# Attention with masked tokens: context of one slot block in four as three float16 products, row additions moved to GpSimd, leaner buffers

## The chip, the cores and the metric

The kernel runs on one core of a Trainium2 chip. TensorE (PE in the profile; its weight loads are PEld) multiplies matrices from SBUF into PSUM. VectorE (DVE), ScalarE (ACT) and GpSimd (POOL) work on tiles of 128 partitions, and SyncE (SP) issues transfers. Every engine takes its own instructions in order and waits for the others by semaphores. The metric is the device time of one execution in microseconds. Three timed runs of the kernel before took 1044.49, 1047.27 and 1048.94 us, a median of 1047.27 us.

## The reference

There are 16 batches of 512 features by 1024 tokens, with a mask of zeros and ones for each batch, 8 heads of 64, and queries that serve as keys and values too.

```python
xt = jnp.transpose(x, (0, 2, 1))
q = xt @ Wq.T
qh = q.reshape(B, T, NH, dk).transpose(0, 2, 1, 3)
scores = scale * jnp.einsum('bhqd,bhkd->bhqk', qh, qh)
logits = (scores * cmask + (1.0 - cmask) * NEG) * rmask
attn = jax.nn.softmax(logits, axis=-1)
ctx = jnp.einsum('bhqk,bhkd->bhqd', attn, qh)
out = ctx.transpose(0, 2, 1, 3).reshape(B, T, D) @ Wo.T
return x + transpose(out)
```

A masked key gets no weight. A masked query has logits of zero throughout, so that its context is the mean of all values, one row for the whole batch.

## The kernel before

**Work is kept to the active tokens.** About half of a batch's 1024 tokens are active (502 to 539). The kernel sorts them on the chip into slots: `slots` and `index` make for each batch a list of rows, and GpSimd gathers rows of x by an indirect transfer (`rows`, L395). A batch has four slot blocks of 128 and a tail of up to 32 slots; the width A of a batch is 544 (batches 0 to 4), 528 (5 to 13) or 512 (14 and 15). The masked rows get only the mean's row added: they are gathered (`late`), the row `ub` is added (`rest`, L888, on VectorE), and they are scattered to the output (`scatter_now`, L901).

**Stages of a batch.** `xt` transposes the gathered rows on TensorE and splits them into a high and a low float16 part (L444, L445). `query` multiplies with the split weights in three float16 products (L513). `qsplit` splits the queries in the same way into `hl` (L529, L530), copies the high part behind the low one (L531), and four SP transfers (`spread`) bring high and low over each other into `xx`, so that one score needs two products. `value` transposes the queries into `v`, four blocks of 128 slots by 128 (two heads), and takes their squares for the softmax shift; `bottom` turns the largest square into `nm`, the negative shift of each head. `scores` makes one block (128 slots by A) of one head in two PSUM buffers (L701), and ScalarE takes the exponential into a float32 tile `p` and sums it (L705). The symmetry of scores makes this block its own transpose, so it can be used as it is.

**Context.** `attend` multiplies the values of a block with the exponentials of that block and accumulates over the blocks into `pav` (L726): for each half g of the columns (A/2 each) and each head k of a pair, a float32 product of 128 rows, 64 columns of weights and A/2 moving columns. The two heads go to the two halves of the array's columns. The tail's part comes last (L730). Then ScalarE copies `pav` out (L734), `norm` scales and splits it (L799 to L807), `project` multiplies with the output weights (L817), `plus` adds the result to the gathered rows (L822), and GpSimd scatters them.

**Order.** The loop in `run` goes over the batches; within one over 16 pairs (p, i) of a pair of heads p and a block i, with two more places for the tails. At each place the scores of head 2p and of head 2p+1 are made, and `fill` puts units of other stages between them, from a list with costs: projection of the batch before, queries of the batch after, and so on. The context of the four blocks of a pair is made in one group, at the place i = 1 of the next pair, in the order of blocks 3, 2, 1, 0. One transfer of GpSimd is issued at each place (`issue`); it, and the additions of L888, wait for the most recent product of TensorE at the time of writing (`beat`), which paces them. The framework then orders each engine's instructions by its own estimate; `behind` and `high_priority` are hints to it.

**Buffers** that matter here: two in PSUM for scores (`pss`), two small ones in PSUM (`pm`) that queries, projections, transposes and values share, 12 tiles `p`, 6 tiles `v`, 2 tiles `hl` with three parts.

**A guard.** The shift must lie between MMIN and MMAX, the counts of active tokens between 384 and A, and so on (`ok`); otherwise a general path computes the whole again.

Of the kernel before, what the change touches and what calls it, by code (L numbers as in the profile page):

```python
# [10 lines left out]
F32 = mybir.dt.float32  # L11
# [8 lines left out]
P = 128  # L20
D = 512
# [15 lines left out]
MMAX = 60.0  # L37
# [6 lines left out]
HPO = 300  # L44


class Fast:
# [45 lines left out]
    def setup(self, mask_t):  # L93
# [30 lines left out]
        self.oht = fixed("oht", [P, B, TB, NB], F16)  # L124
# [11 lines left out]
        self.qt = fixed("qt", [P, 2, HG, CT])  # L136
        self.number = iota("number", [P, B - 2], [[1, B - 2]], 2, 0)
# [70 lines left out]
    def permute(self):  # L208

        nc, B = self.nc, self.B - 2  # L210
        at, mh = self.at16, self.later16
        each = self.sb([P, B, TB, B], F16, "ch", 2)
        nc.vector.tensor_tensor(each, at.unsqueeze(2).broadcast_to([P, B, TB, B]),
                                mh.rearrange("p b j -> p j b").unsqueeze(1).broadcast_to([P, B, TB, B]), ALU.mult)
        with nc.allow_low_precision(reason="one of the terms is 0 or 1, the others are 0"):
            nc.vector.tensor_reduce(self.later16, each, AX.X, ALU.add)
# [15 lines left out]
    def slots(self, b0, b1):  # L232
# [13 lines left out]
        for j in range(TB):  # L246
# [22 lines left out]
                                self.ionb.unsqueeze(1).broadcast_to([P, NC, NB]), ALU.is_equal)  # L269
        for b in range(B):  # L270
            nc.vector.tensor_tensor(self.oht[:, b0 + b], oh[:, b * TB:(b + 1) * TB, :],
                                    self.tok.unsqueeze(2).broadcast_to([P, TB, NB]), ALU.mult)
# [46 lines left out]
    def index(self, b):  # L319
        nc = self.nc  # L320
        s = self.st[b]
        ol = s["ol"]
        pi = self.pm([P, NB])
        for j in range(TB):
            self.pe = nc.tensor.matmul(pi, lhsT=ol[:, j, :], rhs=self.oht[:, b, j, :], start=(j == 0), stop=(j == TB - 1)).ins
# [78 lines left out]
    def gather_now(self, b, j):  # L404
        s = self.st[b]
        if j < 4:
            s["xa"].append(self.rows(s["idx"][:, j:j + 1], self.sb([P, D], F32, "xa", 13)))
        else:
            s["xt"] = self.rows(s["idx"][:s["A"] - 512, 4:5], self.sb([P, D], F32, "xt"))
# [64 lines left out]
    def xt(self, b, k):  # L474
# [4 lines left out]
        if n:  # L479
            x = s["xa"][k] if k < 4 else s["xt"]  # L480
            if b == 0:
                pt = self.ps_s.tile([P, 2, D], F32, tag="s", name="pss")[:, 0, :DC * n].rearrange("p (c n) -> p c n", c=DC)
            else:
                pt = self.pm([P, DC, n])
            for c in range(DC):
                self.pe = nc.tensor.transpose(pt[:, c, :], x[:n, c * P:(c + 1) * P], self.ident[:n, :n]).ins
# [34 lines left out]
    def qsplit(self, b, e):  # L521
# [5 lines left out]
        full = self.sb([P, 3, C], F16, "hl", 2)  # L527
# [3 lines left out]
        nc.vector.tensor_copy(hl[:, 2, :], hl[:, 0, :])  # L531
# [6 lines left out]
        def spread():  # L538
            lo, up = slice(0, DK), slice(DK, P)
            nc.sync.dma_start(out=xx[lo, 0:2, :], in_=hl[lo, 0:2, :])  # L540
            nc.sync.dma_start(out=xx[up, 0:2, :], in_=hl[lo, 1:3, :])
            nc.sync.dma_start(out=xx[lo, 2:4, :], in_=hl[up, 0:2, :])
            self.last_xx = nc.sync.dma_start(out=xx[up, 2:4, :], in_=hl[up, 1:3, :]).ins
# [15 lines left out]
    def value(self, b, e):  # L559
# [72 lines left out]
    def bottom(self, b, g):  # L632
# [6 lines left out]
        nc.vector.tensor_scalar(nm[:, :HG], pb, -SCALE, None, ALU.mult)  # L639
# [4 lines left out]
        nc.vector.tensor_scalar(okm, nm[:, :HG], -MMAX, None, ALU.is_ge)  # L644
        nc.vector.scalar_tensor_tensor(okm, nm[:, :HG], -MMIN, okm, ALU.is_le, ALU.mult)
# [15 lines left out]
    def scores(self, b, p, i):  # L661
# [8 lines left out]
        if i is None:  # L670
# [8 lines left out]
            t = self.sb([P, C], F32, "p", 12)[:, :A]  # L679
# [24 lines left out]
        t = self.sb([P, C], F32, "p", 12)[:, :A]  # L704
# [3 lines left out]
        return t  # L708

    def attend(self, b, p, i, ps):  # L710
# [6 lines left out]
        for g in range(2):  # L717
            for k in (1, 0) if i < 4 else range(2 if A == C else 1):
                cols = slice(g * CH, (g + 1) * CH)
                if i < 4:  # L720
                    with ExitStack() as st:
                        if self.group_first:

                            st.enter_context(self.behind(self.group_first))
                            st.enter_context(self.tc.high_priority(offset=HPO))
                        mm = nc.tensor.matmul(s["pav"][k * DK:(k + 1) * DK, g, :CH], lhsT=s["v"][p][:, i, k * DK:(k + 1) * DK],  # L726
                                              rhs=ps[k][:, cols], start=(i == 3), stop=(i == 0 and A == 512))
                    self.group_first = self.group_first or mm.ins
                elif A > 512:
                    nc.tensor.matmul(s["pav"][:, g, :CH], lhsT=s["vt"][p // 2][:, k, p % 2 * 2:p % 2 * 2 + 2, :],  # L730
                                     rhs=s["pt"][:, p % 2, cols], start=False, stop=(k == 1 or A < C))
        if i == 4:
# [44 lines left out]
    def norm(self, b, p):  # L777
# [4 lines left out]
        if p == 0:  # L782

            s["ch"] = self.sb([P, NP, 512], F16, "ch", 2) if b < self.B - 1 else self.xh[:, :, :512]
            s["cl"] = self.sb([P, NP, 512], F16, "cl", 2) if b < self.B - 1 else self.xl[:, :, :512]
# [15 lines left out]
        ch, cl = s["ch"][:, p, :], s["cl"][:, p, :]  # L801
# [7 lines left out]
    def product(self, ch, cl, cols, po=None, es=range(DC)):  # L809
# [5 lines left out]
        for e in es:  # L815
            for k, (a, w) in enumerate(((ch, wh), (ch, wl), (cl, wh))):
                nc.tensor.matmul(po[:cols.stop - cols.start], lhsT=a[:, e, cols], rhs=w[:, e, :],  # L817
# [14 lines left out]
    def late(self, b, j, tag="xi", bufs=8):  # L832

        self.post(lambda: self.late_now(b, j, *(("xg", 1) if j == 4 else (tag, bufs))), urgent=j == 4)

    def late_now(self, b, j, tag, bufs):
        s = self.st[b]
        idx = s["tails"][:len(self.group[b]) * CT] if j == 4 else s["idx"][:P if j < 8 else T - self.kept[b] - 3 * P, j:j + 1]
        s.setdefault("xi", {})[j] = self.rows(idx, self.sb([P, D], F32, tag, bufs)), idx

    def project_tail(self, b, *part):
# [6 lines left out]
        po = self.product(*s["ct"], slice(0, m), *part)  # L848
# [8 lines left out]
    def project_means(self, b):  # L857
# [9 lines left out]
        po = self.product(m[:, 0], m[:, 1], slice(0, n))  # L867
# [14 lines left out]
    def rest(self, b, j):  # L882
        s = self.st[b]

        def add():
            x, idx = s["xi"][j]
            n = idx.shape[0]
            self.once(self.nc.vector.tensor_tensor(x[:n], x[:n], s["ub"][:n], ALU.add), self.beat)  # L888
# [414 lines left out]
```

## Time and profile before

| | |
|---|---|
| median of three timed runs | 1047.27 us (1044.49 to 1048.94) |
| the profiled execution's own time | 1036.56 us |
| its span, first to last instruction | 1034.9 us |
| granted TensorE clock, mean | 0.993 |
| TensorE busy | 989.3 us, 96% |
| VectorE busy | 724.1 us, 70% |
| ScalarE busy | 659.2 us, 64% |
| GpSimd busy | 301.5 us, 29% |

The span is cut into instructions of each engine. A busy TensorE is not the same as a TensorE at its peak, because its products overlap: a product's recorded duration is the time from its start to the arrival of its result, and the distance between the starts of two products is what each really costs. "Idle before" is the time that the engine stood still right before the instructions of a group, and the name behind the arrow is what ended it. A line Lnnn is a line of the kernel's source. In the list of waits the name before the arrow waited for the name behind it; then come us in total, times, and the longest.

### The profile page before, as it was taken

The page shows a single profiled execution, that of the slowest core. Times are in us where ns is not written, and L with a number is a line of the kernel's source. Part 1 is how long each engine was busy: PE and PEld are TensorE (multiplying, and loading weights), DVE is VectorE, ACT ScalarE, POOL GpSimd, SP SyncE. Part 2 cuts the span into 40 slices and gives each one's busy share as a digit, 9 for nine tenths or more (in the row PEclk, how much of TensorE's full clock was granted, in tenths as well). Part 3 has the DMA queues.
Part 4 walks back from the last instruction along what each step waited for, and adds up shares of the span by engine and source line. Part 5 has one row for each costly group of instructions (what it writes and reads, how often), then busy time and mean ns, then how long its engine had stood idle before and what let it go on. Part 6 is the DMA issues. An engine that isn't in the chain of part 4 may idle for free. (4 is left out here: it accounts for less than half of the span.)

```text
span 1034.9 us, 23506 instructions
## 1 busy us (share of the span) xinstructions
PE 989.3 (96%) x8455; PEld 686.2 (66%) x8455; DVE 724.1 (70%) x2410; ACT 659.2 (64%) x1702; POOL 301.5 (29%) x307
## 2 busy tenths in 40 slices
PE   7798999999999999999999999999999999999996
PEld 6576667666676766767666676766767666676563
DVE  6897668676675667876676787767677776666653
ACT  5876667657667665667667567666667666565550
POOL 3101013222311232333232333323233232326562
PEclk9899999999999999999999999999999999999998
DMA  6846556557654485575658665576665657455652
GB/s 206 224 135 184 139 137 162 174 160 205 175 133 131 138 244 167 154 208 142 197 158 217 181 174 170 155 202 187 164 211 147 195 166 193 140 142 186 195 187 85
DMA packets 78795, 177.73 MB, mean 172 GB/s; under 512 B 14688, under 2 KB 20576, under 8 KB 78672
## 3 DMA queue, kind: packets, MB, share of 16 engines
q1 hardware_dynamic: 57584, 108.40, 39.0%
q0 software_dynamic: 21088, 67.75, 20.9%
q8 instruction: 69, 1.13, 0.5%
q14 instruction: 54, 0.44, 0.1%
HBM read 91.49 MB, written 33.91 MB: 121 GB/s over the span
## 5 line engine op out<-in xcount | busy, mean ns | idle before, releaser
L705 ACT ACTIVATE p<-pss,nm 128x528 f32<-128x528 f32 (+2 forms) x512 | 359.3, 706 | 186.5 <-PE pss L701 176.6
L701 PE MATMUL pss<-xx 128*128 128x264 f16 (+2 forms) x2048 | 302.7, 277 | 6.3 <-ACT p L705 5.2
L726 PE MATMUL pav<-p,v 128*64 128x264 f32 (+2 forms) x2048 | 243.3, 390 | 0.0
L701 PEld LDWEIGHTS <-xx 128*128 128x128 f16 x2048 | 194.9, 99 | 64.2 <-issue 26.2
L726 PEld LDWEIGHTS pav<-p,v 128*64 128x64 f32 x2048 | 141.5, 137 | 85.6 <-issue 13.5
L901 POOL DMA_INDIRECT y_out<-xa,idx x68 | 73.5, 1081 | 282.3 <-PE pss L701 100.1
L513 PE MATMUL pm<-xh,wqh 128*128 128x264 f16 (+5 forms) x512 | 142.4, 278 | 3.7 <-DVE xa L822 3.1
L513 PE MATMUL pm<-xh,wql 128*128 128x264 f16 (+5 forms) x512 | 141.9, 277 | 0.0
L513 PE MATMUL pm<-xl,wqh 128*128 128x264 f16 (+5 forms) x512 | 141.8, 277 | 0.0
L395 POOL DMA_INDIRECT xa<-x_in,idx x68 | 67.4, 992 | 208.2 <-PE pss L701 91.8
L513 PEld LDWEIGHTS <-wqh 128*128 128x128 f16 x1024 | 98.3, 99 | 23.7 <-issue 7.1
L705 ACT ACTIVATION_READ_ACCUMULATOR p<-pss,nm 128x1 f32 x512 | 104.1, 203 | 0.0
L901 POOL DMA_INDIRECT y_out<-xi,idx x60 | 73.6, 1226 | 96.7 <-PE pss L701 27.6
L817 PE MATMUL pm<-woh,ch 128*128 128x512 f16 x240 | 91.1, 380 | 0.0
L817 PE MATMUL pm<-wol,ch 128*128 128x512 f16 x240 | 91.0, 379 | 0.0
L817 PE MATMUL pm<-woh,cl 128*128 128x512 f16 x240 | 91.0, 379 | 0.0
L395 POOL DMA_INDIRECT xi<-x_in,idx x60 | 62.5, 1042 | 93.6 <-PE pss L701 31.2
L516 ACT ACTIVATE q<-pm 128x264 f32<-128x264 f32 (+5 forms) x128 | 50.1, 391 | 58.1 <-PE pm L513 57.4
L822 DVE SCALAR_TENSOR_TENSOR xa<-pm,xa 128x512 f32<-128x512 f32 x60 | 41.3, 688 | 54.3 <-PE pm L817 50.6
L817 PEld LDWEIGHTS <-ch 128*128 128x128 f16 x480 | 46.0, 98 | 44.8 <-issue 0.9
L888 DVE TENSOR_TENSOR xi<-xi,ub 128x512 f32<-128x512 f32 (+1 forms) x60 | 40.8, 687 | 42.6 <-PE pss L701 42.3
L799 DVE TENSOR_TENSOR c<-c,rb 128x528 f32<-128x528 f32 (+2 forms) x64 | 45.4, 709 | 30.0 <-PE pm L513 16.3
(223 smaller groups left out, 1506.4 us busy)
## 6 DMA issues: line engine op xcount, KB each, us to landing
xx<-hl SPq DMA_DIRECT2D x224, 136.0 KB
xm<-x_nat_in SPq DMA_DIRECT2D x56, 512.0 KB
rb<-rd SPq DMA_DIRECT2D x72, 132.0 KB
rb<-rd SPq DMA_DIRECT2D x40, 136.0 KB
pt<-c SPq DMA_DIRECT2D x36, 132.0 KB
pt<-p SPq DMA_DIRECT2D x36, 132.0 KB
ub<-ud SPq DMA_DIRECT2D x16, 256.0 KB
xx<-hl SPq DMA_DIRECT2D x32, 128.0 KB
```

What stands on the lines that cost most here:

```text
L395: dma = self.nc.gpsimd.indirect_dma_start(out=tile[:n], out_offset=None, in_=self.x, in_offset=bass.IndirectOffsetOnAxis(ap=idx, axis=0))
L513: self.beat = nc.tensor.matmul(pq, lhsT=w[:, c, e * P:(e + 1) * P], rhs=xx[:, c, cols], start=(k == 0), stop=(k == 3 * DC - 1)).ins
L516: nc.scalar.activation(s["q"][:, e, cols], pq, AF.Copy, scale=1.0 / (SX * SW))
L701: self.beat = nc.tensor.matmul(pt[:, g, :CH], lhsT=xx[:, 2 * k, i * P:(i + 1) * P], rhs=xx[:, 2 * k + a, g * CH:(g + 1) * CH], start=(a == ...
L705: self.exp = [nc.scalar.activation(t.rearrange("p (g c) -> p g c", g=2), pt[:, :, :CH], AF.Exp, bias=s["nm"][p // HG][:, p % HG:p % HG + 1 ...
L726: mm = nc.tensor.matmul(s["pav"][k * DK:(k + 1) * DK, g, :CH], lhsT=s["v"][p][:, i, k * DK:(k + 1) * DK], rhs=ps[k][:, cols], start=(i == ...
L799: self.once(nc.vector.tensor_tensor(c[:, :A], c[:, :A], s["rb"][p], ALU.mult), self.beat if p < 3 else None)
L817: nc.tensor.matmul(po[:cols.stop - cols.start], lhsT=a[:, e, cols], rhs=w[:, e, :], start=(e == 0 and k == 0), stop=(e == DC - 1 and k == 2))
L822: self.nc.vector.scalar_tensor_tensor(x, po, 1.0 / (SX * SW), x, ALU.mult, ALU.add)
L888: self.once(self.nc.vector.tensor_tensor(x[:n], x[:n], s["ub"][:n], ALU.add), self.beat)
L901: dma = self.nc.gpsimd.indirect_dma_start(out=self.out, out_offset=bass.IndirectOffsetOnAxis(ap=idx, axis=0), in_=x, in_offset=None)
```

## The change

*Context of block 0.* The exponent gets a constant of 26 ln 2 added (LIFT), so the exponentials of all blocks are 2^26 times as large; the correction for empty slots and the sums carry the same factor. For block 0 alone (PARTS), the exponential t is split: ph is t/2048 in float16, on VectorE for even heads and on ScalarE for odd ones, and pl is 2048 ph - t in float16, on VectorE. The value's block 0 is split in `parts`: 2048 v in float16 (ScalarE, out of PSUM), the rest of 2048 v (VectorE), and the negative high part over 2048 (GpSimd). The context of block 0 then is three float16 products in place of a float32 one: high value by ph, low value by ph, negative high value by pl. Blocks 1, 2, 3 and the tail stay as they were.

*Row additions.* The addition of the mean's row to the masked rows (`rest`) goes from VectorE to GpSimd, in line with its transfers.

*Buffers.* 10 tiles `p` for 12; `hl` without the copy of the high part, which two of the four spreading transfers replace by reading the two parts in reverse order; the one-hot tables in two buffers of four batches for one of 16; `ch` and `cl` in six tiles of one pair each; one tile `xgt` for the tails' rows of both kinds, in different partitions; the permutation of masks in two halves. New tiles: `ph` and `pl` (4 each) and `vp` (6).

*Guard.* MMAX goes from 60 to 20.

```diff
-MMAX = 60.0
+MMAX = 20.0
+LIFT = 26.0 * math.log(2.0)
+UP = 2048.0
+PARTS = (0,)
...
-        full = self.sb([P, 3, C], F16, "hl", 2)
+        full = self.sb([P, 2, C], F16, "hl", 2)
...
-        nc.vector.tensor_copy(hl[:, 2, :], hl[:, 0, :])
...
-            nc.sync.dma_start(out=xx[lo, 0:2, :], in_=hl[lo, 0:2, :])
-            nc.sync.dma_start(out=xx[up, 0:2, :], in_=hl[lo, 1:3, :])
+            nc.sync.dma_start(out=xx[lo, 0:2, :], in_=hl[lo])
+            nc.sync.dma_start(out=xx[up, 0:2, :], in_=turned(hl[lo]))
...
+        s.setdefault("vp", []).append(self.parts(v, pv))
...
+    def parts(self, v, pv):
+        nc = self.nc
+        n = len(PARTS)
+        t = self.sb([P, 3, n, P], F16, "vp", 6)
+        nc.scalar.activation(t[:, 0], pv[:, :n], AF.Copy, scale=UP)
+        nc.vector.scalar_tensor_tensor(t[:, 1], v[:, :n], UP, t[:, 0], ALU.mult, ALU.subtract)
+        nc.gpsimd.tensor_scalar(t[:, 2], t[:, 0], -1.0 / UP, None, ALU.mult)
+        return t
...
-        nc.vector.tensor_scalar(nm[:, :HG], pb, -SCALE, None, ALU.mult)
+        nc.vector.tensor_scalar(nm[:, :HG], pb, -SCALE, LIFT, ALU.mult, ALU.add)
...
-        t = self.sb([P, C], F32, "p", 12)[:, :A]
+        t = self.sb([P, C], F32, "p", 10)[:, :A]
...
-        return t
+        if i not in PARTS:
+            return t
+        hi, lo = (self.sb([P, C], F16, k, 4)[:, :A] for k in ("ph", "pl"))
+        if p % 2:
+            nc.scalar.activation(hi, t, AF.Copy, scale=1.0 / UP)
+        else:
+            nc.vector.tensor_scalar(hi, t, 1.0 / UP, None, ALU.mult)
+        nc.vector.scalar_tensor_tensor(lo, hi, UP, t, ALU.mult, ALU.subtract)
+        return hi, lo
...
+            terms = [(v[:, i], ps)]
+            if i in PARTS:
+                terms = [(vp[:, j, i], [h[j // 2] for h in ps]) for j in range(3)]
+            for g in range(2):
+                for j, (w, r) in enumerate(terms):
+                    for k in (1, 0):
...
+                            mm = nc.tensor.matmul(s["pav"][k * DK:(k + 1) * DK, g, :CH], lhsT=w[:, k * DK:(k + 1) * DK],
+                                                  rhs=r[k][:, cols], start=(i == 3),
+                                                  stop=(i == 0 and A == 512 and j == len(terms) - 1))
...
-            self.once(self.nc.vector.tensor_tensor(x[:n], x[:n], s["ub"][:n], ALU.add), self.beat)
+            with self.behind(*(() if self.pool and self.pool[0] in self.scatters else self.pool)):
+                i = self.nc.gpsimd.tensor_tensor(x[:n], x[:n], s["ub"][:n], ALU.add)
+            self.once(i, self.beat)
```

More of the change, by code (lines that the diff above doesn't have):

```diff
@@ L211, in permute @@
         at, mh = self.at16, self.later16
[L212 to L216, printed above, removed]
+        parts = []
+        for k in range(2):
+            n = B // 2
+            each = self.sb([P, n, TB, B], F16, "tmp", 2)
+            nc.vector.tensor_tensor(each, at[:, k * n:(k + 1) * n].unsqueeze(2).broadcast_to([P, n, TB, B]),
+                                    mh.rearrange("p b j -> p j b").unsqueeze(1).broadcast_to([P, n, TB, B]), ALU.mult)
+            parts.append(each)
+        for k, each in enumerate(parts):
+            with nc.allow_low_precision(reason="one of the terms is 0 or 1, the others are 0"):
+                nc.vector.tensor_reduce(mh[:, k * n:(k + 1) * n], each, AX.X, ALU.add)
     def active(self, b0, b1):
@@ L324, in index @@
         for j in range(TB):
-            self.pe = nc.tensor.matmul(pi, lhsT=ol[:, j, :], rhs=self.oht[:, b, j, :], start=(j == 0), stop=(j == TB - 1)).ins
+            self.pe = nc.tensor.matmul(pi, lhsT=ol[:, j, :], rhs=self.oht[b][:, j, :], start=(j == 0), stop=(j == TB - 1)).ins
         s["idx"] = self.sb([P, NB], I32, "idx", 7)
@@ L408, in gather_now @@
         else:
-            s["xt"] = self.rows(s["idx"][:s["A"] - 512, 4:5], self.sb([P, D], F32, "xt"))
+            s["xt"] = self.rows(s["idx"][:s["A"] - 512, 4:5], self.xgt[P - CT:])
     def start(self, b):
@@ L816, in product @@
             for k, (a, w) in enumerate(((ch, wh), (ch, wl), (cl, wh))):
-                nc.tensor.matmul(po[:cols.stop - cols.start], lhsT=a[:, e, cols], rhs=w[:, e, :],
+                nc.tensor.matmul(po[:cols.stop - cols.start], lhsT=a[e][:, cols], rhs=w[:, e, :],
                                  start=(e == 0 and k == 0), stop=(e == DC - 1 and k == 2))
@@ L847, in project_tail @@
         m = n if "ub" in s else n + len(group)
-        po = self.product(*s["ct"], slice(0, m), *part)
+        po = self.product(*([t[:, e] for e in range(DC)] for t in s["ct"]), slice(0, m), *part)
         if m > n:
@@ L866, in project_means @@
             nc.vector.tensor_tensor(m[:, 1, :, k], mq, m[:, 0, :, k], ALU.subtract)
-        po = self.product(m[:, 0], m[:, 1], slice(0, n))
+        po = self.product([m[:, 0, e] for e in range(DC)], [m[:, 1, e] for e in range(DC)], slice(0, n))
         us = self.sb([P, D], F32, "tmp", 2)
```

55 lines of the change are left out of this document (31 added, 24 removed).

## The prediction

> **What bounds the kernel now.** I read the busy shares first, then the waits of TensorE, then single stretches of its timeline, then the groups by shape.
>
> The shares of the page, three rows of its groups, and the table of stretches:
>
> ```profile
> PE 989.3 (96%) x8455; PEld 686.2 (66%) x8455; DVE 724.1 (70%) x2410; ACT 659.2 (64%) x1702; POOL 301.5 (29%) x307
> ...
> L726 PE MATMUL pav<-p,v 128*64 128x264 f32 (+2 forms) x2048 | 243.3, 390 | 0.0
> ```
> ```profile
> PE pss L701 <- ACT p L705: 5.2, 12, 0.6
> PE pm L764 <- ACT p L705: 4.5, 6, 0.8
> ...
> PE pm L513 <- DVE xa L822: 3.1, 5, 1.0
> PE pm L764 <- DVE rcol L758: 3.1, 4, 0.9
> ```
> TensorE has work 96% of the span, and what it waits for is small: by the whole list of its waits, ScalarE costs it about 12 us and VectorE about 10 us after the start (names first: who waits, then for whom, us, times, longest). So a change pays if it shortens TensorE's own stream, and costs where it makes ScalarE or VectorE late. How long a product takes is not in the mean of 390 ns, which is a latency; it is in the distance of starts:
>
> ```profile
> 401.40 3.78 PE L726 MATMUL pav<-p,v 128*64 128x264 f32 x32
> 405.11 0.38 PE L637 MATMUL pm<-ident,m 128*128 128x4 f32 x2
> ```
> ```profile
> 420.97 0.63 PE L676 MATMUL pss<-xx 128*32 128x264 f16 x16
> 421.53 0.33 PE L764 MATMUL pm<-ident,rcol 128*128 128x128 f32 x1
> ```
> One group of context products is 16 float32 products of 64 columns each, recorded as 32. They run two at a time in the two column halves: the records start in pairs, 222.5 ns from pair to pair, so 16 rounds, 3.56 us, and 0.15 us until the next work starts. The float16 group of 32-column products (L676) is the nearest row to what comes: four products start within 10 ns, the next four 111.5 ns later. So a round of float16 is half a recorded float32 round, and a float32 product takes two of those.
>
> The other engines, and the stretch in which VectorE is fullest (PE, PEld, DVE, ACT, POOL busy us, then clock and DMA):
>
> ```profile
> 40.00:80.00 40.00, 37.98 (x325) 26.75 (x327) 37.18 (x119) 30.43 (x82) 1.27 (x1) 0.92 0.56 150
> 80.00:140.00 60.00, 56.84 (x498) 40.16 (x497) 40.32 (x134) 39.93 (x105) 6.00 (x6) 1.00 0.54 146
> 200.00:900.00 700.00, 683.45 (x5920) 476.50 (x5921) 498.17 (x1696) 459.73 (x1184) 202.21 (x194) 1.00 0.62 174
> ```
> ```profile
> L888 DVE TENSOR_TENSOR xi<-xi,ub 128x512 f32<-128x512 f32 x46 | 31.2, 689 | 42.6 <-PE pss L701 42.3 <-DMA ub<-ud 0.3
> ...
> L530 DVE TENSOR_TENSOR hl<-q,hl 128x528 f16<-128x528 f32 x36 | 25.3, 704 | 0.2
> ...
> L529 DVE CAST hl<-q 128x528 f16<-128x528 f32 x36 | 15.5, 432 | 0.3 <-DVE q L519 0.2
> ...
> L531 DVE COPY hl<-hl 128x528 f16<-128x528 f16 x36 | 10.4, 290 | 0.0
> ```
> From 200 to 900 us TensorE is 98% busy, VectorE 71%, ScalarE 66%, GpSimd 29%. From 40 to 80 us VectorE is 93% busy.
>
> **The change, part by part.** The sum is made against the profiled execution: span 1034.9 us, 1036.56 us in all, which is 10.7 us below the median of the timed runs (1047.27). I carry the difference over to the median.
>
> *Context of block 0 on TensorE.* There are 64 groups (16 batches, 4 pairs of heads). In each, block 0 was 4 float32 products, 4 recorded rounds of 222.5 ns, 890 ns. It becomes 12 float16 products, two halves at a time, 6 rounds of 111.5 ns, 669 ns. That is 221 ns less; at 272 columns 4 x 229.1 - 6 x 115.5 = 223 ns (20 groups), at 256 columns 4 x 215.9 - 6 x 107.9 = 216 ns (8 groups, the half of the float32 round). Sum: 36 x 0.221 + 20 x 0.223 + 8 x 0.216 = 14.2 us off. All of it is on the path. Going from float32 to float16 inside the group is a step the trace lacks: nothing at best; at worst another 95 ns, as the end of both column-tiled groups costs beyond their last round, 6.1 us. The tiling does not change there, so I take near nothing, 1 us.
>
> A round also loads weights: 2 x 64 columns now, 4 x 32 in L676, 128 either way, and L676 shows its loads (92 to 97 ns each) starting while its products run, with the rounds still 111.5 ns apart. Here a rule speaks against the change. The Trainium skill ("TensorE: Matmul & The Clock Gate", sections "LDWEIGHTS" and "Part 3: Packing small matmuls — row/col tiling") has weight loads overlap running products only where the row group differs, and a load take its columns divided by 1.2 GHz. All these products use all rows, so by it a round would be an estimated 111 + 2 x 53 = 218 ns, the block 1.31 us, and the kernel 27 us slower. The rounds of L676 disagree, so I leave it 3 in 100.
>
> *VectorE.* Added: 128 residuals pl (two float32 inputs, float16 out, as L530, 0.704) 90 us; 64 quotients ph for even heads, as the cast L529, 0.432 (bounds: copy L531 0.29, L530 0.70), 28 us; 64 small vp (as L519, 128x144, 0.30) 19 us. Gone: 64 row additions, 44 us, and 64 copies L531, 18.6 us. Net +74 us: 70% becomes about 78%. The additions also left VectorE idle for 46.7 us until TensorE's beat came; that blocking goes too. Cover: ph and pl of block 0 are first needed a step later, at the end of the group, behind the 12 float32 products of blocks 3, 2 and 1 (2.7 us). What queues behind them on VectorE is the release of TensorE's two small PSUM buffers (L822, L445); pl of an odd head also waits for ScalarE's quotient, and holds these up meanwhile.
>
> *ScalarE.* Added: 64 quotients for odd heads (as L552, 128x512 in 0.639) 42 us, 64 vp out of PSUM (between L650, 5 elements, 0.205, and L516, 264, 0.390; by the slope of L516 to L572 0.28) 18 us. 64% becomes 70%. Behind them wait the exponentials, which free the scores' PSUM.
>
> *GpSimd.* Added: 64 additions and 64 small multiplications. The trace has no two-input operation there. Its select over 128x128 float32 takes 0.283, its one-element memset 0.098, which gives 0.84 for 512 elements of one input; below it the memset's slope gives 0.49, above it twice the select's 1.6. I take 1.1, nearer to the select. With 0.29 for a multiplication that is 89 us: 29% becomes 38%. Behind an addition stand gathers and scatters, paced by TensorE's beats: between 200 and 900 us GpSimd idles 498 of 700. At the end, 8 additions come after 985 us, 8 x 1.4 = 11 us with the gaps; GpSimd idles 12.5 us before the last four scatters (from 1026 us, they wait for VectorE), so I count nothing; at 1.6 the end would move by 3 us.
>
> *SP and buffers.* The copy of the high half goes, and two of the four spreading DMAs read it in reverse order: 8192 packets more at no more than the queue's mean 0.11 us, over 16 engines under 57 us each, 62% to 67% of DMA. TensorE waited 2.9 us for these transfers once, so 0 to 1 us; taken as nothing. Exponentials have 10 buffers for 12, and block 0's come free once split instead of last, so I see no later start. The shared tile for tails uses different partitions; the permutation is the same work in two halves; the raised exponent fills a free slot of existing instructions. All 0.
>
> *What TensorE loses.* In the first batch the splits of three pairs, 3 x 1.83, and four vp, less four copies, put 5.5 us into a VectorE that had 2.8 us free in 40. Bounds 0 and 5.5 us; from 80 us on VectorE is 67% busy and catches up, so I take 2. Afterwards the 22 us of waits for ScalarE and VectorE grow as their idle shares shrink (29% to 22%, 36% to 30%): times 1.2 to 1.3, 5 us more, from which I take half back for the additions that no longer block VectorE: 2.5. Bounds: 3 us fewer and, doubled, 22 us more.
>
> Sum: -14.2 + 1 + 2 + 2.5 = -8.7 us: 1026.2 us of span, 1038.6 us median.
>
> **Rivals.** *All of it arrives.* No wait grows, the additions' leaving gives 1 to 3 us more: 1030 to 1033. For it: TensorE's real waits are 2% of the middle, and VectorE mostly waits for TensorE, not the reverse. 1 in 10.
>
> *It is eaten up.* VectorE at 78% and in order, with splits that wait for ScalarE, is late for the small PSUM buffers often enough to cost 9 to 14 us: about 1044. For it: the 93% stretch. 2 in 10.
>
> *Slower: GpSimd holds up VectorE.* The trace shows the two touching: GpSimd's descriptor work takes 0.96 us mostly, 1.4 to 1.7 us beside L316 or L530, and a cast L802 beside it 0.58 instead of 0.43. If an addition holds VectorE for half its time, 0.5 us, and all of that reaches TensorE, 64 x 0.5 - 14.2 gives +18, 1065 us; it decides from 0.22 us for each addition. Against it: VectorE's idle time lies between. 13 in 100. The Trainium skill ("SBUF — State Buffer", "Who interferes with whom") calls it an exclusive lock: a GpSimd instruction that reads SBUF and a VectorE instruction with two SBUF inputs, or a copy, cast or tensor_scalar in a two-port mode, fully block each other. The rows just named agree that they touch; none shows a full stop.
>
> *Slower: float16 halves do not run together* (or their loads show). 12 x 111.5 ns is 448 ns more for each block, +28.7 us, 1076. Against it: both L676 and L726 run theirs together. 5 in 100, the 3 above among them.
>
> *The fallback.* The limit on the shift falls from 60 to 20. The largest shift that these inputs give is 16.7, so the general path stays unused.
>
> **How the numbers follow.** The forecast has 52 in 100. A change under 0.5% (5.2 us) cannot be told from none. Faster: 52 + 10 = 0.62; same: 0.20; slower: 0.13 + 0.05 = 0.18. The forecast alone spans 1033 to 1042. The range reaches below to all of the gain with relief, 1030, above into the first slower case, 1060; some 13 in 100 lie outside.
>
> **What would show it.** In the profile after, block 0 as six rounds of about 112 ns, and the group's distance to the next work 3.5 us for 3.7; VectorE near 78%, ScalarE 70%, GpSimd 38%. It is wrong if TensorE's waits for VectorE or ScalarE more than double, if the products with ph start one by one, or if the additions on GpSimd take above 2 us and VectorE's instructions beside them lengthen.

## The result, and the profile after

The changed kernel takes 1094.48 us (median of 4 runs, 1084.39 to 1096.97) beside 1046.55 us before: 1.0437 times, with a 95% interval from 1.0378 to 1.0496. It is slower, by over five times what the forecast had it gain. Its profiled execution took 1084.39 us with a span of 1082.4, against 1036.56 and 1034.9 before: 47.5 us more. Chips differ: the kernel before took between 1035 and 1048 us on those used below, so what counts of a run is its ratio to the runs of before on the same chip.

The shares of the page of after:

```profile
PE 990.2 (91%) x8711; PEld 695.9 (64%) x8711; DVE 860.3 (79%) x2540; ACT 709.5 (66%) x1830; POOL 425.9 (39%) x435
```
TensorE has fallen from 96% to 91% of a longer span. The shares of VectorE and GpSimd are near the forecast (78% and 38%, of a shorter span), ScalarE's is below it (70%). In microseconds VectorE is 136 us busier, and 74 were expected.

First TensorE's own stream. One group of context products in the timeline of after (start, us, engine and line, tiles, number; PEld are weight loads):

```profile
431.93 2.89 PE L769 MATMUL pav<-p,v 128*64 128x264 f32 x24
434.43 0.79 PEld L769 LDWEIGHTS <-vp 128*64 128x64 f16 x12
434.65 0.40 PE L769 MATMUL pav<-ph,vp 128*64 128x264 f16 x4
434.88 0.28 PE L769 MATMUL pav<-pl,vp 128*64 128x264 f16 x2
434.99 0.40 PE L769 MATMUL pav<-ph,vp 128*64 128x264 f16 x4
435.22 0.28 PE L769 MATMUL pav<-pl,vp 128*64 128x264 f16 x2
435.43 0.43 PEld L499 LDWEIGHTS pm<-ident,xa 128*128 128x128 f32 x4 [0.20 <-DVE rcol L798]
```
The group starts at 431.93 and the next work at 435.43: 3.50 us where it was 3.71. The twelve float16 products go in six pairs, two rounds in 0.23 us, one in 0.11, and so on. Taken over all 64 groups, from the start of a group to the start of the next work and without the waits, the stream is 13.8 us shorter. So the gain is there. What eats it are the waits of TensorE (who waits, for whom; us, times, longest):

```profile
PE pm L526 <- DVE xa L864: 15.3, 7, 4.3
PE pss L725 <- ACT p L729: 10.1, 14, 2.2
PE pm L337 <- DVE rr L808: 8.5, 6, 1.5
PE pm L582 <- DVE xl L457: 6.3, 7, 1.3
PE pm L805 <- DVE rcol L799: 5.8, 5, 1.9
```
Added up over the whole list (without the warming products), TensorE waits 55.5 us for VectorE, where it waited 13.9; for ScalarE 13.6, where it was 12.1; for transfers 8.8 and 9.2. The product that waits for the release of a PSUM buffer by L864 (L822 of before) had 3.1 us in 5 places and has 15.3 in 7. It is VectorE alone that has become late, and by few, long waits.

The waits on the list (42.7 us more) and the shorter stream (13.8 us) make 29 of the 47.5 us. Of the other 19, 4 are idle gaps of TensorE that the list doesn't name. Up to 7 go with the clock, an estimate from the granted clock of the two spans (0.987 for 0.993): between the first 30 us and its last products TensorE was granted half the clock for 20.6 us, and for 6.9 in before. The last 8 lie in the time that counts as busy, and were not taken apart.

What VectorE does meanwhile is in the timeline. A stretch of after, VectorE and GpSimd, and the TensorE product behind it:

```profile
406.32 1.68 DVE L849 TENSOR_TENSOR ctl<-c,cth 128x32 f16<-128x32 f32 x1
...
406.67 1.28 POOL L931 TENSOR_TENSOR xi<-xi,ub 128x512 f32<-128x512 f32 x1
...
409.54 1.63 DVE L596 SCALAR_TENSOR_TENSOR vp<-v,vp 128x128 f16<-128x128 f32 x1
...
409.73 1.28 POOL L931 TENSOR_TENSOR xi<-xi,ub 128x512 f32<-128x512 f32 x1
...
412.11 1.99 DVE L646 TENSOR_TENSOR smcol<-smcol,sdt 128x4 f32<-128x4 f32 x1
...
412.79 1.28 POOL L931 TENSOR_TENSOR xi<-xi,ub 96x512 f32<-96x512 f32 x1
...
417.42 0.27 PE L526 MATMUL pm<-xh,wqh 128*128 128x264 f16 x1 [2.48 <-DVE xa L864]
```
A subtraction over 128x32 takes 1.68 us (a median of 0.18), a maximum over four elements 1.99 us (0.15), a small residual 1.63 (0.29). Each of them is over shortly after an addition on GpSimd is over. The last of them began 0.68 us ahead of the addition, while GpSimd still wrote descriptors, and so stood longer than the addition lasts. The delay stays in VectorE's queue until L864, which frees a PSUM buffer, and TensorE stands for 2.48 us. For every VectorE instruction that lies beside one of the 64 additions, its duration less the median of those of its own line, shape and tiles that lie beside none is its excess: 73 us in sum, 41.5 of it in TENSOR_TENSOR, 16.8 in SCALAR_TENSOR_TENSOR, 13.2 in TENSOR_SCALAR, and −0.1 in 13 TENSOR_REDUCE. That is enough for the 62 us by which VectorE is busier than expected. The additions themselves keep to their time:

```profile
L931 POOL TENSOR_TENSOR xi<-xi,ub 128x512 f32<-128x512 f32 x46 | 58.2, 1277 | 1.2 <-issue 0.6
L597 POOL TENSOR_SCALAR vp<-vp 128x128 f16<-128x128 f16 x64 | 44.0, 687 | 76.3 <-ACT vp L595 62.2 <-DVE xl L457 6.5 <-DMA pt<-p 5.8
```

Where on the way the time is lost: the first group of context products of batch 1 starts 13.1 us later than in before (116.1 us), that of batch 2 again 13.1, of batch 5 15.7, of batch 9 27.4, of batch 12 35.8, and the last group 47.2. The first 13 us come before any addition: the earliest starts at 206.6 us.

### The profile page after: what moved, and what is told of

It reads as the page before. It is cut to its first block, busy times and chain, and to the rows that moved or that the text cites. A ratio compares the mean times of both kernels' runs of the same rounds, so it can differ in the third digit from the quotient of the medians.

```text
span 1082.4 us, 24400 instructions
## 1 busy us (share of the span) xinstructions
PE 990.2 (91%) x8711; PEld 695.9 (64%) x8711; DVE 860.3 (79%) x2540; ACT 709.5 (66%) x1830; POOL 425.9 (39%) x435
## 5 line engine op out<-in xcount | busy, mean ns | idle before, releaser
L769 PE MATMUL pav<-p,v 128*64 128x264 f32 (+2 forms) x1536 | 186.3, 392 | 0.0
L526 PE MATMUL pm<-xh,wqh 128*128 128x264 f16 (+5 forms) x512 | 144.2, 282 | 23.2 <-DVE xa L864 15.3
L769 PEld LDWEIGHTS pav<-p,v 128*64 128x64 f32 x1536 | 104.8, 137 | 65.8 <-issue 14.1
L526 PE MATMUL pm<-xl,wqh 128*128 128x264 f16 (+5 forms) x512 | 143.7, 281 | 0.2 <-DVE xl L457 0.2
L526 PE MATMUL pm<-xh,wql 128*128 128x264 f16 (+5 forms) x512 | 143.7, 281 | 0.0
L407 POOL DMA_INDIRECT xa<-x_in,idx x68 | 75.4, 1108 | 157.2 <-PE pss L725 73.3
L526 PEld LDWEIGHTS <-wqh 128*128 128x128 f16 x1024 | 99.9, 100 | 45.7 <-issue 27.7
L739 DVE SCALAR_TENSOR_TENSOR pl<-ph,p 128x528 f16<-128x528 f16 (+2 forms) x128 | 92.4, 724 | 6.3 <-ACT ph L736 5.8
L839 DVE TENSOR_TENSOR c<-c,rb 128x528 f32<-128x528 f32 (+2 forms) x64 | 54.4, 851 | 44.3 <-DMA rb<-rd 15.4
L945 POOL DMA_INDIRECT y_out<-xi,idx x60 | 64.5, 1074 | 44.1 <-issue 20.9
L864 DVE SCALAR_TENSOR_TENSOR xa<-pm,xa 128x512 f32<-128x512 f32 x60 | 41.2, 687 | 50.4 <-PE pm L859 46.6
L931 POOL TENSOR_TENSOR xi<-xi,ub 128x512 f32<-128x512 f32 (+1 forms) x60 | 76.0, 1276 | 1.4 <-issue 0.6
```

What stands on the lines that cost most here:

```text
L407: dma = self.nc.gpsimd.indirect_dma_start(out=tile[:n], out_offset=None, in_=self.x, in_offset=bass.IndirectOffsetOnAxis(ap=idx, axis=0))
L526: self.beat = nc.tensor.matmul(pq, lhsT=w[:, c, e * P:(e + 1) * P], rhs=xx[:, c, cols], start=(k == 0), stop=(k == 3 * DC - 1)).ins
L739: nc.vector.scalar_tensor_tensor(lo, hi, UP, t, ALU.mult, ALU.subtract)
L839: self.once(nc.vector.tensor_tensor(c[:, :A], c[:, :A], s["rb"][p], ALU.mult), self.beat if p < 3 else None)
L864: self.nc.vector.scalar_tensor_tensor(x, po, 1.0 / (SX * SW), x, ALU.mult, ALU.add)
L931: i = self.nc.gpsimd.tensor_tensor(x[:n], x[:n], s["ub"][:n], ALU.add)
```

## The experiments

Three theories stood at the start. P: GpSimd's additions stop VectorE. L: the splitting itself, on VectorE and ScalarE, makes TensorE late. S: the changed buffers, DMAs and order cost by themselves.

**One part at a time.** The first run puts the additions back:

```
-            with self.behind(...):
-                i = self.nc.gpsimd.tensor_tensor(x[:n], x[:n], s["ub"][:n], ALU.add)
-            self.once(i, self.beat)
+            self.once(self.nc.vector.tensor_tensor(x[:n], x[:n], s["ub"][:n], ALU.add), self.beat)
```

> The changed kernel with the row additions back on VectorE, nothing else undone. Theory P (each GpSimd addition stops VectorE's two-input instructions beside it, and TensorE waits for VectorE): most of what grew after 180 us goes, some 30 of 48 us; time over before 1.010 to 1.018. Theory L (VectorE's own splits make it late): the additions come back to VectorE as 44 us more of work and the old waits for the beat, so no gain or worse: 1.040 to 1.055. Theory S (fewer buffers and the new order of instructions): about as the changed kernel, 1.035 to 1.045.

Measured: 1.019 (1.0163 to 1.0217), and on another chip, as e12 below, 1.0156 (1.0132 to 1.018). More than half of the loss goes with the additions, about as P expected, but not all: with TensorE's stream 14 us shorter the kernel is still slower than before. VectorE's excess beside GpSimd's multiplications is 3.9 us over 181 instructions, 0.17 us at most. TensorE's waits for VectorE fall from 55.5 to 25.6 us. The second run also takes the last GpSimd arithmetic away:

```
-        nc.gpsimd.tensor_scalar(t[:, 2], t[:, 0], -1.0 / UP, None, ALU.mult)
+        nc.scalar.activation(t[:, 2], t[:, 0], AF.Copy, scale=-1.0 / UP)
```

> As e1_adds_back, and the third part of the values (negative high part over 2048) made on ScalarE instead of GpSimd, so that GpSimd computes nothing beside its transfers. Theory P: VectorE's instructions have the lengths of before everywhere; 2 to 8 us faster than e1_adds_back, over before 1.004 to 1.014. Theory L: ScalarE gets 18 us more, no gain over e1_adds_back. Theory S: same as e1_adds_back.

Measured: 1.0153 (1.0102 to 1.0204), not to be told from the run before it. What the small multiplication on GpSimd costs, if anything, is too small to show here; the further gain that P expected is not shown. The third goes the other way, the kernel before with nothing but the additions moved:

```
-            self.once(self.nc.vector.tensor_tensor(x[:n], x[:n], s["ub"][:n], ALU.add), self.beat)
+            with self.behind(...):
+                i = self.nc.gpsimd.tensor_tensor(x[:n], x[:n], s["ub"][:n], ALU.add)
+            self.once(i, self.beat)
```

> The kernel before with nothing changed but the row additions, which go to GpSimd. Theory P: slower, since each of the 64 additions stops VectorE for up to 1.3 us; VectorE is less full than in the changed kernel, so 10 to 30 us: 1.010 to 1.030. Theory L: VectorE gets 44 us lighter and no longer idles for the beat: 0.995 to 1.000. Theory S: 1.000.

Measured: 1.0312 (1.0284 to 1.0339), the upper end of what P expected, with all of the context in float32. VectorE's excess beside the additions is 62 us. TensorE's waits for VectorE are 40.9 us for 13.9, and the longest are those of after (L513 is after's L526, L325 its L337):

```profile
PE pm L513 <- DVE xa L822: 15.0, 7, 4.4
PE pm L325 <- DVE rr L767: 8.5, 6, 1.5
```
Its last context group is 32.3 us late, that of e1 13.6 us; the sum, 45.9, is about what the changed kernel shows, 47.2 (by the ratios 3.1% and 1.6 to 1.9%, beside 4.4%). Two causes, which about add up. The fourth has the buffers, transfers and tables of after, without splits and with the additions on VectorE:

```
-PARTS = (0,)
+PARTS = ()
...
-        s.setdefault("vp", []).append(self.parts(v, pv))
```

> The changed kernel without the split (all four blocks float32, as before) and with the additions back on VectorE: what is left are the leaner buffers, the spreading transfers without the copy, and the raised exponent. Theories P and L: 0.995 to 1.003. Theory S: above 1.010.

Measured: 1.0002 (0.9988 to 1.0016). S has fallen: the buffers, the DMAs that turn the halves around, and the halved permutation cost nothing.

**The products and the splitting apart.** The float16 products without the work that makes their parts:

```
-        t = self.sb([P, C], F32, "p", 10)[:, :A]
+        t = (self.sb([P, C], F16, "ph", 8) if i in PARTS else self.sb([P, C], F32, "p", 10))[:, :A]
...
-        nc.vector.scalar_tensor_tensor(lo, hi, UP, t, ALU.mult, ALU.subtract)
-        return hi, lo
+        return t
...
-                terms = [(vp[:, j, i], [h[j // 2] for h in ps]) for j in range(3)]
+                terms = [(self.vc, ps)] * 3
```

> The changed kernel with the additions on VectorE and without the work of splitting: block 0's exponential is written as float16 by the instruction that makes it, all three products of block 0 take this one tile and a constant tile of ones, and no part of the values is made. Left out: the low halves and the values' parts, so the context of block 0 is not the reference's. TensorE's order is that of the changed kernel, VectorE's and ScalarE's work that of the kernel before (some 0.7 us less per block 0 than in the split). Theory L (the three products themselves are as short as planned, the time is lost in waits for the splitting): 0.983 to 0.992 of before, TensorE's 14 us arrive. Rival T (what is lost lies in the float16 products, in loads or in the float32-to-float16 change): 1.005 to 1.02, about as with the additions put back.

Measured: 0.9886 (0.9854 to 0.9917), by this ratio 11.9 us less than before's 1048.08 on that chip, and the interval (9 to 15 us) holds the 14.2 of the forecast's first term. The chip flatters it perhaps: e8 below, timed beside it, was 0.4% better there than on another chip. TensorE gains in either case. The other half, all splits made and read by nobody, float32 products (the additions on VectorE; in this and the three other runs of this part the exponents are not raised):

```
-        return hi, lo
+        return t
...
-            if i in PARTS:
-                terms = [(vp[:, j, i], [h[j // 2] for h in ps]) for j in range(3)]
```

> The other half: all splits are made as in the changed kernel (additions on VectorE), but block 0's products take the float32 tiles as before, and the split tiles are read by nobody. Nothing of the computation is left out. TensorE's stream is that of before, and no product waits for a split; VectorE and ScalarE carry all of its work. Theory L: if the loss comes from work queued in front of other work on VectorE and ScalarE, 1.015 to 1.035; if it comes from the products of block 0 waiting for their own halves, 1.000 to 1.008. Rival T: 1.000 to 1.005.

Measured: 1.0197 (1.0156 to 1.0237), 20.6 us. So most of L is not that products wait for their own halves: the work costs although nobody reads what it makes. Not all is explained: e5 and e6 together make 8.7 us, and e1, which has both, is 16 to 20 us slower than before. The waits of TensorE, first without the splitting (e5), then with it and unused (e6):

```profile
PE pss L726 <- ACT p L730: 9.4, 15, 3.2
PE pav L746 <- DMA pt<-p: 3.8, 3, 2.1
...
PE pm L798 <- DVE rcol L792: 1.5, 2, 0.8
```
```profile
PE pss L725 <- ACT p L729: 12.9, 16, 3.9
PE pm L803 <- DVE rcol L797: 7.5, 7, 2.9
PE pav L753 <- DMA pt<-p: 5.8, 7, 2.3
```
The same three products wait: for the exponentials, for the reciprocals of the row sums on VectorE, and for the tails' transfers, which VectorE's own split of the tail starts. Added up, the waits go from 41.2 to 54.9 us. Of the 35 us between the two runs 14 are TensorE's stream, 14 these waits, and some 7 lie in gaps that the list doesn't name.

Which engine? Two runs add a part of the splitting to the kernel with float32 products: the low halves on VectorE, each taken against a constant,

```
+        lo = self.sb([P, C], F16, "pl", 4)[:, :A]
+        nc.vector.scalar_tensor_tensor(lo, self.hc[:, :A], UP, t, ALU.mult, ALU.subtract)
         return t
```

> Float32 products, additions on VectorE, and of the splitting only the 128 low halves on VectorE, each from a constant tile in place of the high half, 128 x 0.705 = 90 us of VectorE; ScalarE and GpSimd do nothing of it, and nobody reads the low halves. Nothing of the computation is left out. If VectorE's queue is what costs: 90 of the 138 us that all splitting adds there, so 1.010 to 1.018. If ScalarE's is: 0.999 to 1.004.

and ScalarE's part:

```
+        if p % 2:
+            nc.scalar.activation(self.sb([P, C], F16, "ph", 4)[:, :A], t, AF.Copy, scale=1.0 / UP)
         return t
...
-        nc.vector.scalar_tensor_tensor(t[:, 1], v[:, :n], UP, t[:, 0], ALU.mult, ALU.subtract)
-        nc.gpsimd.tensor_scalar(t[:, 2], t[:, 0], -1.0 / UP, None, ALU.mult)
```

> Float32 products, additions on VectorE, and of the splitting only ScalarE's part: the high halves of the odd heads, 64 x 0.644 us, and the first part of the values, 64 instructions; VectorE and GpSimd do nothing of it, and nobody reads what is made. Nothing of the computation is left out. If ScalarE's queue is what costs: 1.010 to 1.020. If VectorE's is: 0.999 to 1.004.

Measured: 1.0044 (1.0028 to 1.006) and 1.0054 (1.0032 to 1.0076). Neither expectation met: neither VectorE's low halves nor ScalarE's part costs the 2% alone. The two together make 1.0%; the other half comes with what both runs left out (the even heads' high halves on VectorE, 27 us, and the values' other parts) or with both engines being fuller at once. That was not taken further apart.

**Where in the kernel.** Batch 0 was done with float32 products, the other fifteen as in e1:

```
-        if i not in PARTS:
+        if i not in PARTS or b == 0:
...
-            if i in PARTS:
+            if i in PARTS and b:
```

> The changed kernel with the additions on VectorE and batch 0 done as before (float32 products, no splits in it). Batch 0 lost 8.8 us in the run with all batches split and additions on VectorE, and the batches after it together 6. If this loss stands by itself: 1.007 to 1.013, about 8 us under that run. If the later batches take over what batch 0 gave up (their loads and rows come earlier and are then waited for): 1.015 to 1.02.

Measured: 0.9998 (0.9976 to 1.0021), less than either expectation. By the ratios, leaving one batch of sixteen alone takes back 1.6 to 1.9% of the time; by plain times, 1048.11 us beside 1055.88 and 1050.42 on other chips, 2 to 8 us. In the traces its first group of batch 1 starts at 119.2 us, e1's at 124.0. That batch 0 loses is shown, how much is not. Next the splits only where e1 had on the whole not fallen back, batches 1 to 4 and 13 to 15, with the values' third part on ScalarE:

```
+QUIET = (1, 2, 3, 4, 13, 14, 15)
...
-        if i not in PARTS:
+        if i not in PARTS or b not in QUIET:
```

> Split only in batches 1 to 4 and 13 to 15, the third part of the values on ScalarE, additions on VectorE; the other nine batches as before. In these seven batches the run with the additions put back was up to 1.4 us per batch ahead of before, 3 in all; TensorE's stream is 7 x 0.9 = 6 us shorter. If the loss sits only where tails and row additions crowd VectorE: 0.994 to 0.999. If splitting costs wherever it is: 1.004 to 1.01.

Measured: 0.9927 (0.99 to 0.9955), below either expectation. On the same chip e7, which splits in batches 5 to 12 as well, was at 0.9998. Since before took 1048 us on that chip and 1036 beside e1, this kernel and e1 were run once more, side by side:

> The kernel that splits in batches 1 to 4 and 13 to 15 alone, once more beside before. It was at 0.9927 where before took 1048 us; before took 1036 us beside the run with the additions put back. If the 0.7% is the kernel's, 0.990 to 0.996 again; if it hangs on how long before takes, 0.997 to 1.003 where before takes 1036.

> The changed kernel with the additions on VectorE, once more, beside the one that splits in seven batches: the two differ by nine batches of splitting and by who makes the values' third part. By the first run and by theory L 1.013 to 1.021, 2 to 3 parts in 100 above that one; if what was measured before was a matter of before's time alone, 1.005 to 1.012.

Measured: 0.9969 (0.9954 to 0.9983) and 1.0156 (1.0132 to 1.018). The seven quiet batches make the one version that beats both kernels, by 0.3 to 0.7% (3 to 8 us of time for 7/16 x 14.2 = 6 us of stream). Its VectorE is at 73%. Splitting in the other nine batches as well (with the values' third part on GpSimd, which made no difference that showed in e2) makes it 1.9% slower on the same chip: the same work pays in some batches and costs in others.

**What stops VectorE.** The additions moved to GpSimd could also cost through GpSimd's own queue, or through rows that leave later. So at each of the 64 places an instruction was added that nobody needs, while VectorE kept its additions (buffers as in e4). First a second addition, over constant tiles:

```
             self.once(self.nc.vector.tensor_tensor(x[:n], x[:n], s["ub"][:n], ALU.add), self.beat)
+            with self.behind(...):
+                i = self.nc.gpsimd.tensor_tensor(self.idle[2][:n, :512], self.idle[0][:n, :512],
+                                                 self.idle[1][:n, :512], ALU.add)
+            self.once(i, self.beat)
```

> The kernel with the changed buffers alone (measured at 1.000 of before), rows' additions on VectorE as before, and at each of the 64 places one addition more on GpSimd, from two constant tiles into a third that nobody reads: VectorE keeps all of its work, and nobody waits for the new instruction but what stands behind it on GpSimd. Theory P (GpSimd's reads and VectorE's instructions with two inputs from SBUF stop each other): 1.02 to 1.045, VectorE's two-input instructions and casts beside the additions 60 to 80 us longer in sum. Rival Q (the loss of the moved additions came from GpSimd's own queue, its gathers and scatters behind them, or from rows that leave later): Q by the queue 1.01 to 1.03 too, but with VectorE's instructions beside the additions less than 15 us longer in sum; Q by the rows that leave later 0.998 to 1.004.

then a memset in its place:

```
+                i = self.nc.gpsimd.memset(self.idle[2][:n], 1.0)
```

> The same with a memset of 128x1024 in place of the addition: GpSimd is held for about as long at the same 64 places (by the rows of before, 0.2 us for 128x128, an estimate of 0.8 to 1.6 us), but reads nothing. P: instructions of VectorE with two inputs keep their time; if only reads are shared, 0.999 to 1.006. If casts and copies are stopped by a write too, 1.005 to 1.015, with subtractions and products at their own time. Q by the queue: about what the additional addition costs, 1.01 to 1.03.

Measured: 1.0419 (1.0391 to 1.0446) with the addition, of 1.320 us, and 1.0062 (1.0042 to 1.0082) with the memset, of 0.968 us. GpSimd's queue is held for 84.5 us by the one and 61.9 by the other; the costs differ by a factor of seven. The queue is not it. The same product on VectorE in the two timelines, beside the addition and beside the memset:

```profile
269.00 2.04 DVE L841 TENSOR_TENSOR c<-c,rb 128x544 f32<-128x544 f32 x1 [0.70 <-PE pm L529]
269.16 1.29 POOL L934 TENSOR_TENSOR idle<-idle,idle 128x512 f32<-128x512 f32 x1
```
```profile
268.48 0.73 DVE L841 TENSOR_TENSOR c<-c,rb 128x544 f32<-128x544 f32 x1 [0.70 <-PE pm L529]
268.61 0.97 POOL L934 MEMSET idle<- 128x1024 f32 x1
...
271.59 1.27 DVE L354 TENSOR_SCALAR hr<-row,n 128x144 f32<-128x144 f32 x1
271.81 0.96 POOL L934 MEMSET idle<- 96x1024 f32 x1
```
The product takes 2.04 us beside the addition, its own 0.73 and the addition's 1.29, though its record begins first. Beside the memset it takes 0.73. An instruction with one input (L354, 0.3 us where nothing lies beside it) is stopped by the memset too. By the sums, reckoned as above: beside the 64 spare additions 62 TENSOR_TENSOR are 49.5 us longer and all of VectorE's instructions 72.6; beside the 64 memsets 79 TENSOR_TENSOR are 4.0 us longer, and 32 TENSOR_SCALAR and CAST 26.5 us. VectorE's busy time, in which records that overlap don't count twice, tells the same: 783.1 us beside the additions, 734.7 beside the memsets, 711.4 in e4, which has neither. So stops of 72 us cost 43 us of time and stops of 23 us cost 6: the loss is not in proportion to their sum, and which instructions are stopped matters too. TensorE's waits in the run with spare additions are those of after:

```profile
PE pm L529 <- DVE xa L866: 15.3, 12, 2.7
PE pm L807 <- DVE rcol L801: 11.1, 12, 3.0
PE pm L340 <- DVE rr L810: 9.0, 7, 1.5
```
With 49.5 us of waits for VectorE and VectorE at 73% of the span, this run shows the loss without a float16 product in the context and without the splitting's load.

## Why the prediction was wrong

**The step that failed** is "What TensorE loses", the later waits: 2.5 us with bounds of −3 and +22. They were worked out by scaling 22 us of waits by VectorE's and ScalarE's idle shares, and the additions were even counted as a relief to VectorE. Measured: waits for VectorE went from 13.9 to 55.5 us, those for ScalarE by 1.5. An average idle share says nothing of a stop of 1.3 us in front of an instruction that TensorE needs next. Of the signs that the prediction named for being wrong, the doubled waits came; the sign for GpSimd asked for additions above 2 us, while they took 1.28 and it was VectorE's instructions that became longer.

**The cause was among the rivals, with 13 in 100.** "GpSimd holds up VectorE" named the place, the mechanism and the point from which it decides, 0.22 us for each addition. Its size was 0.5 us, half an addition; measured are 73 us of stops over 64, 1.1 us each, nearly a whole one, and 26 to 32 us of time (after against e1 and e12; e3). The argument against it, that VectorE's idle time lies between, does not hold: each of the 64 additions in after, and 63 of the 64 in e9, lies beside an instruction of VectorE with two inputs, a cast, a copy or a TENSOR_SCALAR. The rows that were at hand (descriptor work of 1.4 to 1.7 us, a cast of 0.58 for 0.43) showed touches between an engine that mostly writes and instructions that mostly read. They bounded nothing about an addition that reads. The rule that was quoted beside them did speak of a full stop. The Trainium skill ("SBUF — State Buffer", "Who interferes with whom") has a VectorE instruction with two SBUF inputs contend with a GpSimd instruction that reads SBUF but not with one that only writes, and copies, casts and tensor_scalar in two-port modes with both, and never a tensor_reduce. The sums above agree: 49.5 us and 4.0 us for TENSOR_TENSOR beside additions and memsets, 26.5 us for casts and TENSOR_SCALAR beside memsets, −0.1 us for TENSOR_REDUCE beside additions. The page also lets whoever issues first finish; here the product of 269.00 was recorded first and waited all the same. GpSimd was then still at descriptors (until 269.13), so the trace doesn't settle which of the two issued first.

**The rivals were taken as exclusive, and two came together.** "It is eaten up", 1044 us, was VectorE late for small PSUM buffers, at 9 to 14 us. e1 shows that the splitting costs more: the kernel is 1.6 to 1.9% slower although TensorE's stream gains 14 us, so some 30 to 34 us are lost. Only a part of this is the VectorE of that rival: of the 21.5 us by which e1's waits exceed those of before, 11.7 are for VectorE, 7.2 for transfers and 2.6 for ScalarE. With the stop, 26 to 32 us, less the 14 us gained, that makes about the 1094.

**The first batch** was a step on its own: 2 us, at most 5.5. By the start of batch 1 the changed kernel was 13.1 us late, e1 7.9, and with batch 0 left alone the kernel of e1 is, by its ratio, back at the time of before (e7). The window from 40 to 80 us of after, whose row of before was shown (busy us of PE, PEld, DVE, ACT, POOL, then clock, DMA share, GB/s):

```profile
40.00:80.00 40.00, 32.70 (x260) 22.77 (x259) 32.08 (x91) 27.16 (x73) 1.90 (x2) 0.87 0.52 133
80.00:140.00 60.00, 51.13 (x472) 36.63 (x471) 49.11 (x163) 42.08 (x110) 10.93 (x11) 1.00 0.55 149
200.00:900.00 700.00, 657.70 (x5864) 464.08 (x5863) 574.46 (x1719) 477.52 (x1230) 276.11 (x273) 1.00 0.60 169
```
VectorE does not become fuller from 40 to 80 us but emptier, 32.1 us for 37.2: added work there was not a matter of fitting 5.5 us into 2.8. It sits in order behind exponentials that now come later. At 46.75 us the cast of the tail, L709, waits 4.68 us for its exponential. The granted clock of this window, 0.87 for 0.92, makes up to 2 us of the delay. The bound of 5.5 was a sum of busy time; that the delay goes round through ScalarE, VectorE and TensorE is how I read these rows, and no run separates it.

**What was right.** TensorE's 14.2 us (13.8 in the stream, and 0.9886 end to end in e5); 1 us for the change of type at most. The rival that float16 halves don't run together, or that their loads show, has fallen by the group above: six rounds, not twelve. There the rule of the Trainium skill ("TensorE: Matmul & The Clock Gate", "LDWEIGHTS" and "Part 3: Packing small matmuls — row/col tiling") would have made the kernel 27 us slower, and e5 was faster by 11.9. The durations of pl (0.705 us in e12, forecast 0.704), ph (0.426, forecast 0.432) and the odd heads' ph on ScalarE (0.644 for 0.639) were right. Two on GpSimd were low: the addition 1.277 us for 1.1, the multiplication 0.687 for 0.29, and no harm of the second showed (e2). Buffers, transfers and tables at 0 were right (e4), and the fallback stayed unused. One reading was off without harm: the list of waits has TensorE wait 2.5 us for the spreading transfers, not 2.9.

## What to carry to other kernels

Before a two-input operation goes from VectorE to GpSimd, look at what VectorE does at that moment: here 64 additions of 1.28 us, taken off VectorE, gave it 62 to 73 us of stops and cost 3.1% (e3). On a unit that works in order, an idle share of 30% does not show that there is room for new work; what counts is what stands behind it when the bottleneck needs a buffer back. A gain that costs another engine time can be taken in part: splitting in the seven quiet batches alone won 0.3 to 0.7%, in all sixteen it lost 1.6 to 1.9%.

## What the runs showed of the hardware

- GpSimd's additions, which read two inputs from SBUF, stop VectorE's two-input instructions for about their whole length: 0.15 us became 1.99, 0.73 became 2.04. They stop TENSOR_SCALAR too (14.3 us over 15 in e9). A memset stops casts and TENSOR_SCALAR (0.3 us became 1.27), but hardly any TENSOR_TENSOR: 4.0 us over 79, most of it in four, each right behind a TENSOR_SCALAR that was stopped. TENSOR_REDUCE keeps its time beside additions (−0.1 us over 13) and nearly keeps it beside memsets (1.2 us over 18).
- The small multiplication over 128x128 float16 stopped nobody for its length: 3.9 us over 181 VectorE instructions in e1, 0.17 us at most. Its own time varies there, from 0.53 us to 1.46.
- With the additions it is VectorE that waits: the additions moved to GpSimd last 1.257 to 1.297 us in after, while VectorE's instructions beside them carry the 73 us. In e9 eight of the 64 spare additions lasted 1.59 to 1.61 us, so there GpSimd may have waited as well.
